# The first five steps of a pipelined attention kernel, with their work in another order

## The chip, the cores and the metric

The kernel runs on one core of a Trainium2 chip. A core has five engines with a queue each, which work through their own instructions in order and wait for one another by semaphores: TensorE (PE; its weight loads are listed as PEld), VectorE (DVE), ScalarE (ACT), GpSimd (POOL) and SyncE (SP), which here issues all transfers. The metric is the device time of one execution in microseconds. Four runs of the kernel before gave 1517.66 to 1519.4 us, median 1518.58 us.

## The reference, cut to what matters

The input x has 16 sequences of 256 tokens with 256 features. The layer is attention with 16 heads of 128, and a feed-forward part whose weights come packed in four bits:

```
x = x + layernorm(attention(layernorm(x)))
x = x + layernorm(ffn(layernorm(x)))
attention:  q, k, v = x W_Q + b_Q, x W_K + b_K, x W_V + b_V     (per head)
            scores = q k / sqrt(128), causal mask, softmax
            out = sum over heads of (softmax v) W_O, + b_O
ffn:        (gelu_tanh(x Wg) * (x Wu)) Wd, weights unpacked from 4 bits and scaled
```

Everything is float32. The kernel keeps that precision by splitting each factor into a rounded high part and the rest, the low part, and adding three products.

## The kernel before

Tokens are taken in blocks of 512 (two sequences), and heads in pairs. A unit is one block with one head; a pair p is one block with two heads, units 2p and 2p+1. There are 128 units. The attention phase is one loop over i from -5 to N+1 (line 1021), a pipeline written out by hand: iteration i works on unit i+5's keys and queries (`st_qk`, line 370), unit i+4's scores and softmax (`st_s`, line 421), its transpose (`st_t`), a fourth part of the values of four heads (`st_v`), the transfers that bring the transposed softmax to the right partitions (`st_w` writes it to DRAM as hop, `st_b` reads it back as pt), the split of pt into ph and pl (`st_p`), the product with the values (`st_z`), and the output product of a finished pair (`st_o`). In the first five iterations most of the later stages have nothing to do yet. From i = 0 on `st_z` runs too, and from the second pair on `st_o`.

Nothing reorders this. The helper `run` (line 95) chains every instruction behind the one emitted before it, and `dma` (line 86) chains every transfer on SyncE, so each engine's order is the order in which the Python code calls. Work that is not part of the pipeline stands in lists of jobs (`splits`, `urgent`, `behind`, `idle` and others). A call of `slot(kinds, lists)` (line 133) advances a counter and lets the first job that is due and of the right kind do one step at that place in the order.

Before the loop the first block's x is normalized, transposed by TensorE and split into xT (`first_tokens`, line 245). TensorE is kept busy meanwhile by transposes of the identity into a tile called warm (`keep_warm`, line 1003).

In `st_qk` six products go into the bank pk; ScalarE adds the bias and writes kh (rounded) and kr (plain), VectorE writes kl, the rest. The same follows with pq, qh, qr and ql. pk and pq have one bank each. In `st_s` TensorE multiplies Q and K into two banks sc, VectorE adds the mask and takes the minima (the scores carry a minus sign) of four pieces, ScalarE takes four exponentials with their sums, VectorE the reciprocals rc in two steps, and GpSimd multiplies pr by them in four. Between the exponentials and the second reciprocal there is a `slot` (line 451). VectorE then transposes pr into tr (`st_t`). `st_v` writes vh by ScalarE and puts VectorE's step for vl into a list called `after`; the next `st_s` runs it behind its minima.

A weight of the first block is split by `w_split` (line 297): ScalarE writes the high part from raw, the low part is written by GpSimd for v and o (all but the first v) and by VectorE for k and q, the next pair's raw is fetched by `w_raw`, and four slots later `w_keep` copies both parts to DRAM, from where later blocks read them. q's weights are multiplied by `qscale` in the same step. `w_get` (line 331) puts such a split on the list `splits`. Before the loop the splits of v's third weight (2) and of k and q for pair 1 are put there, in that order (line 1013); the loop adds k and q of pair p+4 in even iterations, o and v in odd ones. `weights` is the helper that does that (line 1016).

The order in an iteration of the kernel before:

```
if 0 <= i + 4 < N:
    st_s(i + 4)
slot(V_)
if i + 5 < N:
    st_qk(i + 5)
slot(V_, urgent, behind); slot(G_); slot(G_)
if 0 <= i + 4 < N:
    st_t(i + 4)
...  (st_o, st_z, st_p, st_v, st_b, st_w)
weights(...)
slot(A_ + G_)
```

Of the kernel before, what the change touches and what calls it, by code (L numbers as in the profile page):

```python
# [15 lines left out]
ALU = mybir.AluOpType  # L16
# [12 lines left out]
def kernel(  # L29
# [19 lines left out]
    nc = tc.nc  # L49
# [10 lines left out]
    def f(ap):  # L60
        return ap.bitcast(F32)
# [33 lines left out]
    def run(op, dst, *args, **kw):  # L95
        with ExitStack() as behind:
            for m in last.values():
                behind.enter_context(tc.issue_after(m))
            ins = op(dst, *args, **kw)  # L99
        last[ins.ins.engine] = ins.ins  # L100
        return ins
# [3 lines left out]
    V_, G_, A_, N_ = "vgan"  # L105
    urgent, behind, splits, idle, made, spare = (deque() for _ in range(6))
# [3 lines left out]
    def step(jobs, kinds=None):  # L110

        while jobs:
            job, at, kind = jobs[0]
            if kinds and (at > now[0] or kind not in kinds + N_):
                return False
            try:
                to = next(job)
                jobs[0][1:] = (now[0] + to[1], to[0]) if isinstance(to, tuple) else (now[0] + 1, to)
            except StopIteration:
                jobs.popleft()  # L120
            if not kinds or kind != N_:
                return True
        return False

    def add(jobs, job, kind):
        jobs.append([job, 0, kind])

    def overdue(time):
        while late and late[0][0] <= time:
            _, do, args = late.popleft()  # L130
            do(*args)

    def slot(kinds, *lanes):

        now[0] += 1
        overdue(now[0])
        for jobs in lanes or (splits, urgent, behind, made, spare, idle):
            if step(jobs, kinds):
                return
# [149 lines left out]
    def w_tile(n):  # L289
        return wp.tile([P, 2, 1024 if n == "v" else 512], F32R, tag=f"w{n}", name=f"w{n}", bufs=2)  # L290
# [6 lines left out]
    def w_split(p, n):  # L297

        raw = RAW.pop((p, n)).rearrange("p (k c) -> p k c", k=2)
        key, done = p, True  # L300
        if n == "v":
            key, done = p // 2, p % 2
            w = HALF.pop(key) if done else w_tile(n)
            if not done:
                HALF[key] = w
            wv_ = w_view(w)[:, :, :, (p % 2) * 256 : (p % 2 + 1) * 256]
        else:
            w = w_tile(n)
            wv_ = w_view(w)
        c = qscale if n == "q" else 1.0  # L310
        run(nc.scalar.activation, wv_[:, 0], raw, AF.Copy, scale=c)
        if n in "vo" and (p, n) != (0, "v"):
            run(nc.gpsimd.tensor_tensor, wv_[:, 1], raw, f(wv_[:, 0]), ALU.subtract)
        else:
            run(nc.vector.scalar_tensor_tensor, wv_[:, 1], raw, c, f(wv_[:, 0]), ALU.mult, ALU.subtract)
        ahead = p + (2 if n == "v" else 1)
        if ahead < NG:
            w_raw(ahead, n)
        if done:
            W[key, n] = w_view(w)  # L320
            late.append((now[0] + 4, w_keep, (key, n, w)))
# [9 lines left out]
    def w_get(p, n):  # L331

        if p < NG:
            add(splits, split(p, n), A_ if n in "vo" else V_)
        elif p < len(pairs):
            overdue(now[0] + 4)
            if n == "v":
                key, part = p // 2, p % 2
                w = HALF.pop(key) if part else w_tile(n)
                HALF[key] = w  # L340
                dma(f(w[:, part]), WD[key % (NG // 2), n][:, part])
                if part:
                    W[key, n] = w_view(HALF.pop(key))
            else:
                w = w_tile(n)
                dma(f(w), WD[p % NG, n])
                W[p, n] = w_view(w)
# [16 lines left out]
    N = len(units)  # L364
# [3 lines left out]
    after = deque()  # L368
# [52 lines left out]
    def st_s(u):  # L421
        qh, ql, qr = Q.pop(u)
        kh, kl, kr = K.pop(u)
        pr = work.tile([P, 3, 2, P], F32, tag="pr", name="pr")
        mn = small.tile([P, 2, 2], F32, tag="mn", name="mn")
        sm = small.tile([P, 2, 2], F32, tag="sm", name="sm")
        rc = small.tile([P, 2, 2], F32, tag="rc", name="rc")
        parts = ((0, slice(0, 1)), (1, slice(1, 3)))
        scb = []
        for bi in range(2):  # L430
            sc = ps.tile([P, 3 * P], F32, tag="sc", name="sc", bufs=2)
            ks = slice(bi * S, (bi + 1) * S)
            run(nc.tensor.matmul, sc[:, 0:P], qr[:, bi, :], kr[:, bi, :], start=True, stop=True)
            mm3(sc[:, P:], [(lambda a: (qh, ql)[a][:, bi, :], lambda c: (kh, kl)[c][:, ks])])
            for q, cs in ((0, slice(0, P)), (1, slice(P, 3 * P))):
                run(
                    nc.vector.tensor_tensor_reduce,
                    sc[:, cs], sc[:, cs], mask[:, 2 * P - (cs.stop - cs.start) :], scale=1.0, scalar=3.0e38,
                    op0=ALU.add, op1=ALU.min, accum_out=mn[:, bi, q : q + 1],
                )  # L440
            scb.append(sc.rearrange("p (a c) -> p a c", a=3))
        while after:
            run(*after.popleft())
        for bi in range(2):
            for q, cs in parts:
                run(
                    nc.scalar.activation, pr[:, cs, bi, :], scb[bi][:, cs, :], AF.Exp,
                    bias=mn[:, bi, q : q + 1], scale=-1.0, accum_out=sm[:, bi, q : q + 1],
                )
            if bi:  # L450
                slot(V_, splits, idle, urgent, behind)
            run(nc.vector.reciprocal, rc[:, bi, :], sm[:, bi, :])
            for q, cs in parts:
                run(
                    nc.gpsimd.tensor_scalar, pr[:, cs, bi, :], pr[:, cs, bi, :], rc[:, bi, q : q + 1], 1.0,
                    ALU.mult, ALU.mult,
                )
        PR[u] = pr
# [12 lines left out]
    def st_w(u):  # L471
        HOP[u] = dram.tile([P, 4, 6 * 32], F32, tag="hop", name="hop", bufs=4)
        spread(HOP[u], TR.pop(u).rearrange("p k m i -> p k (m i)"))
# [529 lines left out]
    def keep_warm(count):  # L1003
        for n in range(count):
            run(nc.tensor.transpose, warm[:, n % 4, :], ident, ident)

    keep_warm(30)
    add(urgent, first, V_)
    finish(urgent)
    run(nc.gpsimd.tensor_scalar, bqs, bqk[:, 0, :], qscale, 1.0, ALU.mult, ALU.mult)  # L1010
    for p in range(2):
        w_split(p, "v")
    for p, n in (2, "v"), (1, "k"), (1, "q"):
        w_get(p, n)

    def weights(*of):
        for pn, n in of:
# [3 lines left out]
    for i in range(-5, N + 2):  # L1021
        p = i // 2
        odd = i % 2 == 1
        if p >= 0 and not odd and p < len(pairs):
            b, g = pairs[p]
            if g == 0 and b + 1 < NBLK:
                add(urgent, ln1(b + 1), N_)
            if b == 0 and g == 6:
                pieces = [(fg, n) for fg in range(NG) for n in "gud"]
                f_load(*pieces[0])  # L1030
            if b == 0 and g == 7:
                for m, piece in enumerate(pieces):
                    add(idle, f_make(*piece, pieces[m + 1] if m + 1 < len(pieces) else None), V_)
            if b == NBLK - 1 and g == 0:
                add(spare, x_ops(0), N_)
        if 0 <= i + 4 < N:
            st_s(i + 4)
        slot(V_)
        if i + 5 < N:
            st_qk(i + 5)  # L1040
        slot(V_, urgent, behind)
        slot(G_)
        slot(G_)
        if 0 <= i + 4 < N:
            st_t(i + 4)
        if i == N:
            await_(X[0], "last", spare)
            X[0].pop("last")()
        if i >= N - 4:
            part(0, ("m1", "m2", "m6", "m5", "m7", "m3")[i - (N - 4)])  # L1050
        if 0 <= p - 1 < len(pairs):
            st_o(p - 1, i % 2)
        if 0 <= i < N:
            st_z(i)
        if 0 <= i + 1 < N:
            st_p(i + 1)
        if 0 <= i + 4 < N:
            st_v(i + 4)
        elif after:
            run(*after.popleft())  # L1060
        if 0 <= i + 3 < N:
            st_b(i + 3)
        if 0 <= i + 4 < N:
            st_w(i + 4)
        if odd:
            weights((p + 1, "o"), (p + 5, "v"))
        else:
            weights((p + 4, "k"), (p + 4, "q"))
        slot(A_ + G_)
        if N - 9 <= i < N - 7:  # L1070
            f_get(0, "ug"[i - (N - 9)])
# [97 lines left out]
```

## Time and profile before

| | |
|---|---|
| median of four runs | 1518.58 us |
| the profiled execution | 1518.14 us, its span 1516.4 us |
| TensorE busy | 1499.0 us |
| VectorE, ScalarE, GpSimd busy | 1186.4, 1038.4, 731.0 us |
| TensorE busy in 0:10, 10:20, 20:30, 30:40, 40:50 us | 8.36, 7.70, 8.77, 8.82, 10.00 us |
| GpSimd busy in the same | 2.96, 4.64, 3.25, 3.88, 7.28 us |
| share of the 16 DMA engines in the same | 0.73, 0.94, 0.92, 1.00, 1.01 |
| granted TensorE clock | 1.00 in each of these |

The last four rows are busy times in windows of 10 us from the start of the span. Matmuls overlap, so that a busy TensorE is not TensorE at its peak. In a line of the timeline the first number is the start and the second the time in us that the instruction took, or the merged row of several; "xT<-tpx" reads "writes xT from tpx"; what stands in brackets is how long the engine sat idle before it and who ended that. All engines pipeline a little, so that the next instruction may start shortly before the one before it has ended. Nearly every instruction is issued by the helper `run`, and so has line 99; the names of the tiles tell them apart.

### The profile page before, as it was taken

The numbers are of one execution on the slowest core, as the hardware profiler recorded it, in microseconds if no ns is written. First come the engines' busy times: TensorE is split into PE (matmuls) and PEld (weight loads), VectorE is DVE, ScalarE is ACT, GpSimd is POOL, SyncE is SP. The second block draws the span as 40 slices with busy tenths as digits, with TensorE's granted clock in tenths as the row PEclk, the third lists the DMA queues.
The fourth block names the chain that finished last, engine by engine and source line by source line (L and its number), as shares of the span: only waits on it lengthen the run. The fifth ranks groups of instructions, "written<-read, shape, count | busy, mean of one in ns | idle before, by whom it ended". The sixth has DMA issues, their size and how long they took to land.

```text
span 1516.4 us, 25754 instructions
## 1 busy us (share of the span) xinstructions
PE 1499.0 (99%) x7831; PEld 1278.5 (84%) x7831; DVE 1186.4 (78%) x3011; ACT 1038.4 (68%) x2614; POOL 731.0 (48%) x951
## 2 busy tenths in 40 slices
PE   8999999999999999999999999999999999999997
PEld 7888888888888888888888888887888888888886
DVE  6776787787787888788778777777787887787866
ACT  6877766767676677676777767775766665666565
POOL 3755578677667776866876876880000000000000
PEclk9999999999999999999999999999999999999999
DMA  8998899989899899889889999976557465655561
GB/s 300 335 324 260 261 309 309 289 301 309 286 290 329 281 321 301 280 309 314 275 283 321 297 299 317 315 243 263 210 193 262 183 248 196 249 181 195 222 234 57
DMA packets 200426, 407.55 MB, mean 269 GB/s; under 512 B 21472, under 2 KB 128480, under 8 KB 189536
## 3 DMA queue, kind: packets, MB, share of 16 engines
q1 hardware_dynamic: 200288, 405.91, 79.3%
q8 instruction: 62, 1.02, 0.3%
q14 instruction: 76, 0.62, 0.1%
HBM read 294.15 MB, written 111.67 MB: 268 GB/s over the span
## 4 chain that ended last, share of the span: by engine, by line
PE 93%; DVE 2%; DMA 2%; ACT 1%; POOL 1%; issue 1%; SPq 0%; POOLq 0%; DVEq 0%; ACTq 0%
PE pd L99 13%; PE pk L99 11%; PE pv L99 11%; PE pq L99 11%; PE po L99 11%; PE pz L99 10%; PE sc L99 9%; PE pa L99 8%; PE pf L99 5%; PE pe L99 2%; DVE sum L99 1%; DMA wu<-fu 1%; DMA rawq<-in_wq 0%; ACT pr L99 0%; DMA rawv<-in_wv 0%
## 5 line engine op out<-in xcount | busy, mean ns | idle before, releaser
L99 POOL TENSOR_SCALAR pr<-pr,rc 128x128 f32<-128x128 f32 (+1 forms) x512 | 251.5, 507 | 90.3 <-DVE rc L99 90.3
L99 POOL TENSOR_TENSOR rs<-rs,mhalf 128x4 f32<-128x4 f32 (+1 forms) x35 | 34.5, 986 | 485.9 <-DVE rs L99 277.2
L99 ACT ACTIVATE pr<-sc,mn 128x128 f32<-128x128 f32 (+1 forms) x512 | 208.8, 420 | 87.3 <-DVE mn L99 87.3
L99 POOL TENSOR_TENSOR pl<-pt,ph 128x512 fp32r<-128x512 f32 x128 | 165.2, 1291 | 188.6 <-ACT ph L99 184.9
L99 DVE CUSTOM_DVE_ANT_0 sc<-sc,mask 128x128 f32<-128x128 f32 (+1 forms) x512 | 180.7, 373 | 67.8 <-PE sc L99 59.1
L99 PE MATMUL pv<-wv,xT 128*128 128x512 f32 x768 | 208.9, 407 | 0.0
L99 ACT ACTIVATE zh<-pz,bqk 128x512 fp32r<-128x512 f32 x128 | 88.3, 690 | 167.2 <-PE pz L99 167.2
L99 PE MATMUL pk<-xT,wk 128*128 128x512 f32 x768 | 199.5, 395 | 0.3 <-POOL xT L99 0.2
L99 PE MATMUL pd<-inter,wd 128*128 128x512 f32 (+1 forms) x792 | 197.8, 385 | 1.4 <-ACT inter L99 1.0
L99 PE MATMUL pq<-xT,wq 128*128 128x512 f32 x768 | 196.3, 391 | 0.0
L99 PEld LDWEIGHTS pd<-inter,wd 128*128 128x128 f32 x792 | 145.0, 188 | 34.5 <-DVE inter L99 2.9
L99 PEld LDWEIGHTS pq<-xT,wq 128*128 128x128 f32 x768 | 144.2, 188 | 32.9
L99 ACT COPY part<-pa 128x512 f32<-128x512 f32 x192 | 111.9, 586 | 68.7 <-PE pa L99 66.3
L99 PE MATMUL po<-zh,wo 128*128 128x512 f32 x512 | 157.7, 389 | 0.0
L99 PEld LDWEIGHTS pk<-xT,wk 128*128 128x128 f32 x768 | 134.9, 188 | 23.8 <-POOL xT L99 0.7
L99 PEld LDWEIGHTS pv<-wv,xT 128*128 128x128 f32 x768 | 135.0, 189 | 23.6
L99 DVE SCALAR_TENSOR_TENSOR zl<-pz,bqk,zh 128x512 fp32r<-128x512 f32 x128 | 95.9, 749 | 73.4 <-ACT zh L99 73.4
L99 ACT CAST inter<-sum 128x512 fp32r<-128x512 f32 x128 | 80.1, 626 | 87.3 <-DVE sum L99 87.3
L99 DVE TENSOR_TENSOR inter<-sum,inter 128x512 fp32r<-128x512 f32 x128 | 89.1, 696 | 56.9 <-ACT inter L99 55.9
L99 DVE STREAM_TRANSPOSE tr<-pr 128x768 f32<-128x768 f32 x128 | 123.3, 963 | 1.7 <-POOL pr L99 1.2
L99 DVE SCALAR_TENSOR_TENSOR kl<-pk,bqk,kh 128x512 fp32r<-128x512 f32 x128 | 96.1, 751 | 30.8 <-ACT kr L99 27.0
L99 PEld LDWEIGHTS po<-zh,wo 128*128 128x128 f32 x512 | 96.0, 188 | 19.9
(149 smaller groups left out, 3723.7 us busy)
## 6 DMA issues: line engine op xcount, KB each, us to landing
hop<-tr SPq DMA_DIRECT2D x512, 96.0 KB
pt<-hop SPq DMA_DIRECT2D x128, 384.0 KB
wk<-wk SPq DMA_DIRECT2D x64, 512.0 KB
wq<-wq SPq DMA_DIRECT2D x64, 512.0 KB
wo<-wo SPq DMA_DIRECT2D x64, 512.0 KB
wu<-fu SPq DMA_DIRECT2D x32, 1024.0 KB
wg<-fg SPq DMA_DIRECT2D x32, 1024.0 KB
wv<-wv SPq DMA_DIRECT2D x56, 512.0 KB
```

What stands on the lines that cost most here:

```text
L99: ins = op(dst, *args, **kw)
```

## The change

Only the first five iterations (i from -5 to -1), units 0 to 3 of the softmax, and the weights of k and q for pairs 1 to 3 are touched, and the number of warm-up transposes in front.

- In these iterations the products of K and Q for unit i+5 are emitted in front of the scores of unit i+4, no longer behind them. VectorE's steps for vl that the iteration before put into `after` are emitted in front of that.
- Two slots for splits follow behind `st_s`. The slot inside `st_s`, between the exponentials and the second reciprocal, is left out for units 0 to 3.
- For pairs 1 to 3 the low parts of k's and q's weights are written by GpSimd. q's raw weights are first multiplied by `qscale` in place, by one more GpSimd instruction.
- The split of v's third weight is put on the list at the end of iteration -4, and not before the loop. k and q of pair 1 are left on the list before the loop.
- 27 warm-up transposes in place of 30.

```diff
@@ w_split
-        if n in "vo" and (p, n) != (0, "v"):
+        if n in "vo" and (p, n) != (0, "v") or n in "kq" and 1 <= p <= 3:
+
+            if n == "q":
+                run(nc.gpsimd.tensor_scalar, raw, raw, c, 1.0, ALU.mult, ALU.mult)
             run(nc.gpsimd.tensor_tensor, wv_[:, 1], raw, f(wv_[:, 0]), ALU.subtract)
@@ st_s
-            if bi:
+            if bi and u >= 4:
                 slot(V_, splits, idle, urgent, behind)
@@ before the loop
-    keep_warm(30)
+    keep_warm(27)
...
-    for p, n in (2, "v"), (1, "k"), (1, "q"):
-        w_get(p, n)
+    for n in "kq":
+        w_get(1, n)
@@ the loop
+        if i < 0:
+
+
+            while after:
+                run(*after.popleft())
+            st_qk(i + 5)
         if 0 <= i + 4 < N:
             st_s(i + 4)
+        if i < 0:
+            for _ in range(2):
+                slot(V_, splits)
         slot(V_)
-        if i + 5 < N:
+        if 5 <= i + 5 < N:
             st_qk(i + 5)
...
+        if i == -4:
+            w_get(2, "v")
         if odd:
             weights((p + 1, "o"), (p + 5, "v"))
```

## The prediction

> **What bounds the kernel now.** I read the page first. TensorE is busy for all but 17.4 us of the span, so work taken from another engine is worth nothing where TensorE doesn't wait for it.
>
> ```profile
> PE 1499.0 (99%) x7831; PEld 1278.5 (84%) x7831; DVE 1186.4 (78%) x3011; ACT 1038.4 (68%) x2614; POOL 731.0 (48%) x951
> PE 93%; DVE 2%; DMA 2%; ACT 1%; POOL 1%; issue 1%; SPq 0%; POOLq 0%; DVEq 0%; ACTq 0%
> ```
>
> Then I read the waits of the first 50 us (columns: who <- for whom: us, times, longest). The change touches nothing after them. The only wait of TensorE behind the launch is four times for the last part of Q, 4.7 us in all. After 39.17 it runs without a gap worth naming.
>
> ```profile
> PE sc L99 <- ACT qr L99: 4.7, 4, 1.5
> ```
>
> Last, the timeline of one early iteration (i = -1, unit 3's softmax beside unit 4's products).
>
> ```profile
> 33.74 0.27 DVE L99 CUSTOM_DVE_ANT_0 sc<-sc,mask 128x128 f32<-128x128 f32 x1
> ...
> 34.68 0.37 ACT L99 ACTIVATE pr<-sc,mn 128x128 f32<-128x128 f32 x1 [1.64 <-DVE mn L99]
> ...
> 35.63 0.17 DVE L99 RECIPROCAL rc<-sm 128x2 f32<-128x2 f32 x1 [0.27 <-ACT pr L99]
> ...
> 35.89 0.83 POOL L99 TENSOR_SCALAR pr<-pr,rc 128x128 f32<-128x128 f32 x2 [3.84 <-DVE rc L99]
> ...
> 36.28 0.64 ACT L99 ACTIVATE wk<-rawk 128x512 fp32r<-128x512 f32 x1
> ...
> 36.80 0.64 ACT L99 ACTIVATE wq<-rawq 128x512 fp32r<-128x512 f32 x1
> ...
> 37.33 0.69 ACT L99 ACTIVATE kh<-pk,bqk 128x512 fp32r<-128x512 f32 x1
> ...
> 38.42 0.75 DVE L99 SCALAR_TENSOR_TENSOR kl<-pk,bqk,kh 128x512 fp32r<-128x512 f32 x1
> 38.61 0.51 ACT L99 ACTIVATE qr<-pq,bqs 128x256 f32<-128x256 f32 x1
> ...
> 39.17 0.49 PE L99 MATMUL sc<-kr,qr 128*128 128x128 f32 x2 [1.12 <-ACT qr L99]
> ...
> 39.55 0.97 DVE L99 STREAM_TRANSPOSE tr<-pr 128x768 f32<-128x768 f32 x1
> ...
> 39.70 1.29 POOL L99 TENSOR_TENSOR pl<-pt,ph 128x512 fp32r<-128x512 f32 x1 [0.70 <-ACT ph L99]
> ...
> 40.95 1.31 POOL L99 TENSOR_TENSOR wo<-rawo,wo 128x512 fp32r<-128x512 f32 x1
> ...
> 42.59 1.64 POOL L99 TENSOR_SCALAR pr<-pr,rc 128x128 f32<-128x128 f32 x4 [0.34 <-DVE rc L99]
> ```
>
> The ring is: minima, exponentials, the next pair's weights, the next unit's K and Q on ScalarE, scores, minima. Call M(u) the start of unit u's minima. In the trace M(0) to M(5) are 14.02, 21.44, 28.08, 33.74, 40.44 and 46.73. The reader should also see that GpSimd multiplies pr, then has pl and wo, and has room.
>
> **The change part by part.** Step lengths are from rows of the trace: minima to exponentials 0.94 (33.74 to 34.68); exponentials to first reciprocal 0.95, to GpSimd 0.26, its four multiplications 1.64: M to the end of pr 3.79, so the transpose starts 3.9 after M if nothing else holds it. Transpose to the next VectorE step 0.89 (39.55 to 40.44), vl 0.61, kl 0.73, ql 0.40. On ScalarE the exponentials take 1.60, wk and wq 1.05, kh, kr, qh 0.57, 0.36, 0.36, qr 0.51 to its end.
>
> *Three warm-ups fewer.* Thirty weight loads take 5.30 us (1.57 to 6.87), three 0.53. The transposes of x behind them waited for the loads by 0.4, then wait for the layer norm on VectorE. I take 0.2 earlier for the first product (9.01 to 8.8); the ends are 0 and 0.5.
>
> *K and Q in front of the scores.* TensorE now does pk(1), pq(1) before sc(0). pk has one bank, so pk(1) waits for kl(0): kr(0)'s end 11.56 (11.76 less 0.2) plus 0.75 is 12.3. Then pk 1.28 (28.01 to 29.29), the time from pq's first load to qh 1.85 (10.27 to 12.12), qr's end 0.87 later, ql 0.4: M(0) = 16.8, where it was 14.02. This is 2.8 us paid at once. In return the scores no longer wait for Q. But on VectorE, which runs in order, kl and ql of the next unit leave the place where they lay beside GpSimd's multiplications, and stand behind the transpose and in front of the minima. The new ring is 3.9 + 0.89 + 0.73 + 0.40 = 5.92, not the 5.66 of M(2) to M(3) before.
>
> *vl in front.* In i = -3 and -2 the low part of V comes behind the transpose too: 0.61, ring 6.53. M(1) = 16.8 + 6.53 = 23.3. For M(2) ScalarE is longer: exponentials at 24.3, then 1.60, wk and wq 1.05, vh 0.46, wv 0.54, then kh to qr's end 1.80 gives 29.75, and ql: M(2) = 30.2. M(3) = 36.1. Then i = 0 has the old order, scores before products, so M(4) = 36.1 + 3.9 + 0.89 = 40.9 against 40.44. The ring alone loses 0.45.
>
> *v's third weight later.* Before, ScalarE waited 2.2 us for its transfer in front of the first exponentials (they began at 15.70). That wait goes, which is in the sum above: the first transpose would be at 20.7, where it was 20.55. The load that this split issues moves from 12.90 to about 23.4 on SP; its data is used at 46.49.
>
> *Weights split behind the minima, low parts on GpSimd.* k's and q's low parts leave VectorE (0.69 and 0.67, three times), where they stood beside GpSimd's multiplication, and cost it 0.29 (1.12 against 0.83 for a pair). GpSimd gets k's low part at 1.25 (39.70 to 40.95, same shape), q's scaling and q's low part at 1.25. The scaling, 128x512 in place by two constants, isn't in the trace. The nearest row is pr's: 0.37 for 128 and 0.48 for 256 elements in one pair of 0.83, from which I work out 0.69 for 512; the far end is xn's, 1.23 for 256, so 2.46; below is 0.4, two rows of 0.2 as bqs has. I take 0.69, for pr's is the same operation. In i = -5 the three hide behind pk(1), pq(1) (done by 16.7, needed at 17.6 by pk(2)); in i = -3 they end at 30.4, and pq(4) begins at 31.5. In i = -1 nothing hides them: GpSimd runs in order, and pl(0), wo(0) and pr(4) are queued behind. pr(3) ends at 39.9, k's low 41.15, scaling 41.85, q's low 43.1, pl(0) 44.4 (was 41.0), wo 45.65, pr(4) 47.3 (was 44.23). Then transpose, zl (0.63): M(5) = 47.35 + 0.89 + 0.63 = 48.9, against 46.73. TensorE itself is ahead by 1.0 at 42, then waits about 2.2 for pl(0) in pz(0) (its first two products need no pl), so sc(5) starts at 46.9 against 45.58. sc(6) follows M(5) by the old ring: 52.18 + 2.15 = 54.3. By TensorE's own work it would be 53.4, so M(5) decides. From there on the work of TensorE per unit (7.73, 52.18 to 59.91) is longer than the ring, the lag of 2.1 stays, and the later idle time (mostly waits for ACT, DVE and POOL at the change of phase) moves with it.
>
> *SP's queue.* The copies of k and q to DRAM, and q's next load, now wait on SP for GpSimd's low parts. Queued behind are pt and hop: pt(0) is issued at about 30.8 where it was 26.30. With the 5.4 us that it took to land, that is 36.2, and ScalarE wants it at 39.75: hidden, with 3.5 to spare. pt(2) and pt(3) have 5 us each. If that cover goes, every us beyond is a us of delay.
>
> Sum: 2.1 us. The profiled execution's span 1516.4 becomes 1518.5; with the 1.7 around it (1518.14) 1520.2. It was 0.4 below the median 1518.58, so 1520.7.
>
> [...] No row here shows the scaling itself.
>
> **The rivals.** *A, the scores' wait simply goes.* The 4.7 us and the 0.2 of warm-ups are gained: 1513.7. For it: TensorE needs only 5.3 per early unit. Against: VectorE's ring of 5.9 to 6.5. It decides if rings come out at 5.3 or less and pl(0) ends before 42. *B, GpSimd's queue costs nothing,* since its steps overlap or pr(4) isn't last: the ring's 0.45 stays, 1519.0. *C, the scaling is slow:* at 2.46 it adds 1.8 to the same chain, 3.9 in all, 1522.5; from 1.6 on it is slower by over 0.2%. *D, SP's queue:* transfers run at a share of 1.00 from 30 to 40, and if pt(0) lands at 42 in place of 36.2, ScalarE stands 2.2 longer in front of the exponentials of unit 4: 1522.9.
>
> **How the numbers follow.** Forecast 0.48, A 0.12, B 0.14, C 0.18, D 0.08. My three rings may each be off by 0.5, so the forecast's own range is 1519.2 to 1522.3. 0.2% is 3.0 us, about what a measurement of this kernel can tell from no change: under 1515.5 is faster, over 1521.6 slower. A quarter of the forecast (0.12) lies above, with C and D 0.38; A is faster, 0.12; the rest 0.50. The range, 1517.0 to 1523.4, takes in B with its rings' error and C and D nearly whole, and leaves out A and the tails, 0.2.
>
> **What would show it.** Right: scores no longer wait for qr before unit 5; M(0) near 16.8, M(3) near 36; pz waits some 2 us for pl near 42; GpSimd without a gap from pr(3) to pr(4). Wrong: M(3) under 35 or pl(0) done before 42 (then A or B), a scaling over 1.2 us (C), ScalarE idle before ph for a transfer (D).

## The result, and the profile after

The changed kernel takes 1520.66 us (median of 41 runs) where the kernel before takes 1518.93 us (61 runs beside them). The ratio is 1.0011, with an interval of 1.0006 to 1.0015: some 0.9 to 2.3 us slower. The forecast was 1520.7 us, and a time within 0.2% of before as the likeliest outcome, at 0.50. Both hold. The steps in between held less evenly, and two of them were wrong.

The page of the changed kernel, its busy times and the shares of its chain:

```profile
PE 1500.2 (99%) x7828; PEld 1279.2 (84%) x7828; DVE 1182.2 (78%) x3005; ACT 1038.5 (68%) x2614; POOL 739.6 (49%) x960
PE 93%; DVE 3%; ACT 1%; POOL 1%; issue 1%; DMA 1%; SPq 0%; POOLq 0%; DVEq 0%; ACTq 0%
```

Nine more instructions on GpSimd, six fewer on VectorE (its share of the chain went from 2% to 3%) and three transposes fewer on TensorE: the change does what it says. The waits of the first 55 us (who <- for whom: us in total, times, longest) show what became of TensorE's wait for Q, which was four times and 4.7 us:

```profile
DVE tr L99 <- POOL pr L99: 5.5, 5, 1.7
...
PE sc L99 <- ACT pr L99: 2.2, 1, 2.2
...
PE pv L99 <- DVE vl L99: 1.1, 2, 0.8
...
PE sc L99 <- ACT qr L99: 0.8, 1, 0.8
...
PE pz L99 <- POOL pl L99: 0.3, 1, 0.3
```

The scores no longer wait for Q in the first five units. In their place VectorE waits five times for GpSimd's multiplications, and TensorE waits for the exponentials (the scores of unit 4 need the bank that those of unit 3 still hold), for vl, and for Q once more at unit 6. One ring, on VectorE, as the prediction describes it (unit 1's transpose to unit 2's minima; behind each line in brackets is the idle time before it):

```profile
26.84 0.98 DVE L99 STREAM_TRANSPOSE tr<-pr 128x768 f32<-128x768 f32 x1 [0.97 <-POOL pr L99]
27.75 0.65 DVE L99 TENSOR_TENSOR vl<-pv,vh 128x512 fp32r<-128x512 f32 x1
28.70 0.75 DVE L99 SCALAR_TENSOR_TENSOR kl<-pk,bqk,kh 128x512 fp32r<-128x512 f32 x1 [0.30 <-ACT kr L99]
29.43 0.48 DVE L99 SCALAR_TENSOR_TENSOR ql<-pq,bqs,qh 128x256 fp32r<-128x256 f32 x1
29.83 0.29 DVE L99 CUSTOM_DVE_ANT_0 sc<-sc,mask 128x128 f32<-128x128 f32 x1
```

vl, kl and ql now stand between the transpose and the minima, and the 0.30 in front of kl is ScalarE being longer in this one ring. GpSimd's queue from unit 3's multiplications to unit 4's:

```profile
37.77 1.64 POOL L99 TENSOR_SCALAR pr<-pr,rc 128x128 f32<-128x128 f32 x4 [4.12 <-DVE rc L99]
39.38 1.29 POOL L99 TENSOR_TENSOR wk<-rawk,wk 128x512 fp32r<-128x512 f32 x1
40.75 0.62 POOL L99 TENSOR_SCALAR rawq<-rawq 128x512 f32<-128x512 f32 x1
41.45 1.28 POOL L99 TENSOR_TENSOR wq<-rawq,wq 128x512 fp32r<-128x512 f32 x1
42.70 1.28 POOL L99 TENSOR_TENSOR pl<-pt,ph 128x512 fp32r<-128x512 f32 x1
43.94 1.28 POOL L99 TENSOR_TENSOR wo<-rawo,wo 128x512 fp32r<-128x512 f32 x1
45.20 1.64 POOL L99 TENSOR_SCALAR pr<-pr,rc 128x128 f32<-128x128 f32 x4
```

There is no gap in it, and what follows it on VectorE starts as soon as it is done:

```profile
46.87 0.98 DVE L99 STREAM_TRANSPOSE tr<-pr 128x768 f32<-128x768 f32 x1 [1.67 <-POOL pr L99]
47.77 0.71 DVE L99 SCALAR_TENSOR_TENSOR zl<-pz,bqk,zh 128x512 fp32r<-128x512 f32 x1
48.40 0.29 DVE L99 CUSTOM_DVE_ANT_0 sc<-sc,mask 128x128 f32<-128x128 f32 x1
```

So M(5) is 48.40, where it was 46.73. The first weight load of the scores of unit 6 follows it by 5.45 us in both kernels, and from there the changed kernel stays behind by 1.67 us through the whole attention phase.

In units of the prediction, the starts of the minima:

| | M(0) | M(1) | M(2) | M(3) | M(4) | M(5) |
|---|---|---|---|---|---|---|
| before | 14.02 | 21.44 | 28.08 | 33.74 | 40.44 | 46.73 |
| predicted | 16.8 | 23.3 | 30.2 | 36.1 | 40.9 | 48.9 |
| after | 16.74 | 23.05 | 29.83 | 35.60 | 40.35 | 48.40 |

The new order pays 2.7 us at M(0), earns it back by M(4), and loses it again between M(4) and M(5), behind GpSimd.

One thing in this trace is in no part of the prediction: TensorE's granted clock. The windows of 5 us (length, busy us and instructions of PE, PEld, DVE, ACT and POOL, then the clock, the share of the DMA engines, GB/s):

```profile
35.00:40.00 5.00, 2.83 (x15) 2.16 (x14) 3.07 (x13) 3.43 (x12) 2.23 (x5) 0.93 0.93 337
40.00:45.00 5.00, 4.72 (x21) 3.73 (x19) 3.25 (x13) 4.24 (x14) 4.83 (x5) 0.73 0.96 332
```

Behind the wait of 2.2 us in front of the scores of unit 4 the clock was granted at 0.50, from 39.27 to 42.69. The products of K and Q for unit 5 took 2.54 and 2.15 us in that stretch:

```profile
37.53 0.49 PE L99 MATMUL sc<-kr,qr 128*128 128x128 f32 x2 [2.17 <-ACT pr L99]
...
39.02 2.54 PE L99 MATMUL pk<-xT,wk 128*128 128x512 f32 x6
41.37 2.15 PE L99 MATMUL pq<-xT,wq 128*128 128x512 f32 x6
...
44.03 0.39 PE L99 MATMUL pz<-pl,vh 128*128 128x256 f32 x1 [0.28 <-POOL pl L99]
```

Two theories came out of this. The first is the prediction's: the rings on VectorE set M(0) to M(4), and GpSimd's queue sets M(5) and with it the lag. The second: the half clock, or the new gap in front of it, sets the lag, and GpSimd's queue only happens to end at the same time. A third question was what each part of the change is worth by itself.

### The profile page after: what moved, and what is told of

It is laid out like the page before. It is cut to its first block, busy times and chain, and to the rows that moved or that the text cites. A ratio compares the mean times of both kernels' runs of the same rounds, so it can differ in the third digit from the quotient of the medians.

```text
span 1517.2 us, 25756 instructions
## 1 busy us (share of the span) xinstructions
PE 1500.2 (99%) x7828; PEld 1279.2 (84%) x7828; DVE 1182.2 (78%) x3005; ACT 1038.5 (68%) x2614; POOL 739.6 (49%) x960
## 4 chain that ended last, share of the span: by engine, by line
PE 93%; DVE 3%; ACT 1%; POOL 1%; issue 1%; DMA 1%; SPq 0%; POOLq 0%; DVEq 0%; ACTq 0%
PE pd L99 13%; PE pk L99 11%; PE po L99 11%; PE pq L99 11%; PE pv L99 11%; PE pz L99 10%; PE sc L99 9%; PE pa L99 8%; PE pf L99 5%; PE pe L99 2%; DVE sum L99 1%; PE warm L99 0%; POOL pr L99 0%; DMA hop<-tr 0%; ACT pr L99 0%
```

## The experiments

Each kernel was timed beside the kernel before on the same chip. The lag is how much later the kernel does the same instruction in the attention phase than the profiled run of before does. Profiled runs start between 0.2 us earlier and 0.9 later than that of before, and not at one moment even where the code up to there is the same; the lag below has that taken off, by the first kh of each run (for the changed kernel 1.67 becomes 1.85). Lags and M come from one profiled run each, medians and ratios from the timed runs. The two don't always agree: the lag of e4_scores_first is -0.99 and its median 2.85 below before, the lag of e2_lows_vector 1.60 and its median 0.29 above. So a difference of less than 2 us between two of these kernels rests on the lag, where their intervals overlap.

| kernel | M(3) | M(4) | M(5) | lag | median, us | before beside it | ratio, 95% |
|---|---|---|---|---|---|---|---|
| changed | 35.60 | 40.35 | 48.40 | 1.85 | 1520.66 | 1518.93 | 1.0011, 1.0006 to 1.0015 |
| e1_pair3_vector | 35.85 | 41.58 | 47.86 | 1.09 | 1519.19 | 1519.38 | 0.9998, 0.9989 to 1.0007 |
| e2_lows_vector | 36.23 | 41.96 | 48.25 | 1.60 | 1519.67 | 1519.38 | 1.0002, 0.9993 to 1.0011 |
| e3_lows_alone | 34.00 | 40.69 | 47.11 | 0.59 | 1520.84 | 1519.38 | 1.0009, 1.0001 to 1.0018 |
| e4_scores_first | 32.05 | 37.71 | 46.03 | -0.99 | 1516.53 | 1519.38 | 0.9982, 0.9973 to 0.9991 |
| f1_pair3_later | 32.04 | 37.70 | 45.02 | -0.47 | 1517.32 | 1519.58 | 0.9987, 0.9978 to 0.9996 |
| f2_pair3_later_gpsimd | 31.59 | 37.25 | 43.90 | 1.97 | 1521.13 | 1519.58 | 1.0013, 1.0004 to 1.0022 |
| f3_scaling_thrice | 36.29 | 41.04 | 50.50 | 3.30 | 1522.10 | 1519.58 | 1.0016, 1.0007 to 1.0025 |
| f4_vl_behind | 41.77 | 46.51 | 54.55 | 7.96 | 1525.65 | 1519.58 | 1.0046, 1.0034 to 1.0059 |
| g1_pair3_old_place | 31.51 | 38.20 | 44.48 | -2.07 | 1517.20 | 1519.38 | 0.9987, 0.9978 to 0.9996 |
| g2_v4_later | 30.77 | 37.46 | 43.74 | -1.93 | 1516.87 | 1519.38 | 0.9987, 0.9978 to 0.9996 |
| g3_gap_filled | 35.92 | 40.66 | 48.69 | 1.82 | 1520.82 | 1519.38 | 1.0011, 1.0002 to 1.0020 |
| g4_v_later_alone | 33.23 | 39.93 | 46.22 | -1.37 | 1518.04 | 1519.38 | 0.9994, 0.9985 to 1.0003 |

### Does GpSimd's queue set the end? Two scalings more in it

The first theory says that every us added in front of pl(0) and pr(4) comes out at the end.

```diff
@@ w_split of the changed kernel
                 run(nc.gpsimd.tensor_scalar, raw, raw, c, 1.0, ALU.mult, ALU.mult)
+                for _ in range(2 if p == 3 else 0):
+                    run(nc.gpsimd.tensor_scalar, raw, raw, 1.0, 1.0, ALU.mult, ALU.mult)
```

> The changed kernel with two more multiplications by one of the same size behind q's scaling, for pair 3 alone. Theory G, that the chain of GpSimd from pr(3) to pr(4) sets M(5) and with it the end: each costs 0.69 to 0.71, M(5) 49.8 instead of 48.4, 1.4 us slower than the changed kernel, 3.1 slower than before. If another engine sets it, no change against the changed kernel.

The same stretch of GpSimd's timeline:

```profile
41.45 2.04 POOL L99 TENSOR_SCALAR rawq<-rawq 128x512 f32<-128x512 f32 x3
43.58 1.28 POOL L99 TENSOR_TENSOR wq<-rawq,wq 128x512 fp32r<-128x512 f32 x1
44.81 1.27 POOL L99 TENSOR_TENSOR pl<-pt,ph 128x512 fp32r<-128x512 f32 x1
46.03 1.28 POOL L99 TENSOR_TENSOR wo<-rawo,wo 128x512 fp32r<-128x512 f32 x1
47.30 1.64 POOL L99 TENSOR_SCALAR pr<-pr,rc 128x128 f32<-128x128 f32 x4
```

Two scalings more are 1.42 us more (2.04 against 0.62). The lag grew by 1.45, from 1.85 to 3.30. The chain pr, low parts, pl, wo, pr sets M(5), one for one, and M(5) sets the lag. The medians, 1522.10 against 1520.66, each beside its own runs of before, agree with this, but the intervals of their ratios overlap.

### Does the half clock set it? The gap filled

```diff
@@ the loop of the changed kernel, iteration 0
+        if i == 0:
+            keep_warm(18)
         if 0 <= i + 4 < N:
             st_s(i + 4)
```

> The changed kernel with 18 transposes of the identity in the gap of TensorE in front of sc(4). Theory G: the granted clock stays 1.00, pk(5) and pq(5) take 1.5 each instead of 2.5 and 2.15, but pz(0) then waits about 2 us for pl(0) instead of 0.3; M(5) stays 48.4 and the time is the changed kernel's. Rival C, the half clock costs: M(5) and the time fall by 1.5 us.

With 18 transposes in the gap, the granted clock is 1.00 in both windows, where the changed kernel had 0.93 and 0.73. The windows of this run:

```profile
35.00:40.00 5.00, 4.83 (x35) 4.15 (x34) 3.08 (x13) 3.12 (x12) 1.90 (x5) 1.00 0.98 335
40.00:45.00 5.00, 3.14 (x17) 2.55 (x17) 3.25 (x12) 4.56 (x15) 4.83 (x5) 1.00 0.98 336
```

and TensorE's timeline (the view begins at 36, and 16 of the 18 transposes are in it):

```profile
35.77 1.91 PE L99 MATMUL warm<-ident 128*128 128x128 f32 x16
...
39.34 1.54 PE L99 MATMUL pk<-xT,wk 128*128 128x512 f32 x6
40.72 1.52 PE L99 MATMUL pq<-xT,wq 128*128 128x512 f32 x6
...
44.33 0.39 PE L99 MATMUL pz<-pl,vh 128*128 128x256 f32 x1 [1.86 <-POOL pl L99]
```

K's and Q's products take 1.54 and 1.52 again, and TensorE spends what this saves waiting for pl(0): 1.86 in place of 0.28. The lag is 1.82, that of the changed kernel, and so is the ratio, 1.0011. The second theory falls: the half clock filled a wait that was there anyway.

### Without GpSimd's low parts

One kernel gives only pair 3's low parts back to VectorE, the other those of all three pairs.

```diff
@@ w_split, e1_pair3_vector
-        if n in "vo" and (p, n) != (0, "v") or n in "kq" and 1 <= p <= 3:
+        if n in "vo" and (p, n) != (0, "v") or n in "kq" and 1 <= p <= 2:
@@ w_split, e2_lows_vector
-        if n in "vo" and (p, n) != (0, "v") or n in "kq" and 1 <= p <= 3:
+        if n in "vo" and (p, n) != (0, "v"):
```

> The changed kernel, but the low parts of k and q for pair 3 on VectorE again (pairs 1 and 2 stay on GpSimd). Theory G, GpSimd's queue in iteration -1 makes the lag: GpSimd goes from pr(3) straight to pl(0), pl(0) ends near 41.2 instead of 44.0 and pr(4) near 44.9 instead of 46.8; VectorE pays two low parts in front of the transpose, M(4) 41.1 instead of 40.35; M(5) 47.4 instead of 48.4, sc(6) 52.85 instead of 53.85; about 1.0 us faster than the changed kernel, 0.7 slower than before. Rival C, the half clock of TensorE from 39 to 43 makes the lag: the gap before sc(4) stays, so the clock falls again, M(5) stays 48.4 and the time is the changed kernel's.

> The changed kernel, but all low parts of k and q on VectorE again, no scaling: the new order alone. Theory G: VectorE pays 0.4 in iteration -3 and 0.75 in -1, M(2) 30.2, M(4) 41.5, M(5) 47.8, about 1.05 slower than before and 0.6 faster than the changed kernel. If GpSimd's low parts were the only fault of the change, this one would be faster than before. If they were no fault, it would be slower than the changed kernel by the 1.4 per pair on VectorE, 2 us or more.

GpSimd's queue in e1_pair3_vector ends earlier (pl(0) at 41.90, pr(4) at 45.36), and yet the lag falls only from 1.85 to 1.09. Its timeline shows why, first GpSimd's:

```profile
38.02 2.62 POOL L99 TENSOR_SCALAR pr<-pr,rc 128x128 f32<-128x128 f32 x4 [4.12 <-DVE rc L99]
40.61 1.29 POOL L99 TENSOR_TENSOR pl<-pt,ph 128x512 fp32r<-128x512 f32 x1
```

and VectorE's at the same time:

```profile
39.09 0.69 DVE L99 SCALAR_TENSOR_TENSOR wk<-rawk,wk 128x512 fp32r<-128x512 f32 x1 [0.35 <-ACT wk L99]
39.70 0.68 DVE L99 SCALAR_TENSOR_TENSOR wq<-rawq,wq 128x512 fp32r<-128x512 f32 x1
40.68 0.98 DVE L99 STREAM_TRANSPOSE tr<-pr 128x768 f32<-128x768 f32 x1 [0.30 <-POOL pr L99]
```

While VectorE writes two low parts, GpSimd's four multiplications take 2.62 us and not 1.64. The first three of the four take 1.16 us in the changed kernel (1.64 less the 0.48 of the last), which here would end them at 39.18, 0.09 behind the start of VectorE's first low part; so the excess of 0.98 lies in the fourth, by this estimate. The four end at 40.64, 0.26 behind the second low part. The transpose waits for them, so M(4) is 41.58 and not 40.35. Low parts on VectorE make the ring longer; low parts on GpSimd make the queue in front of M(5) longer. In e2_lows_vector the slow multiplications come in two iterations (2.62 at 25.29 and at 38.40) and the lag is 1.60, almost that of the change. The three kernels' times lie too near each other to be told apart by their intervals; by the medians alone e1 and e2 lie 1.5 and 1.0 us below the change.

### GpSimd's low parts alone

```diff
@@ w_split of the kernel before
-        if n in "vo" and (p, n) != (0, "v"):
+        if n in "vo" and (p, n) != (0, "v") or n in "kq" and 1 <= p <= 3:
+            if n == "q":
+                run(nc.gpsimd.tensor_scalar, raw, raw, c, 1.0, ALU.mult, ALU.mult)
```

> The kernel before, only with the low parts of k and q for pairs 1 to 3 on GpSimd, with the scaling. Theory G: in the old order the splits begin before the products of Q, so GpSimd has k's low part between its multiplications and q's behind them, beside kl and ql; T(u) is still held by ql; pl(0) ends near 42.3 where pz(0) asks for it at 43.4, pr(4) near 45.2; M(5) 46.8, no change within 0.3 us. If GpSimd's 3.2 us per pair cost in any order, it is 1.5 us or more slower than before.

In the old order k's low part lies between the two pairs of multiplications, where GpSimd had room. pr(4) ends at 45.55 (before 44.23), and the lag is 0.59. Most of it doesn't come from there: with the start taken off, M(1) is 0.29 late and M(2) to M(4) are 0.46 to 0.47 late, and pr(4) adds 0.13 to that. The expectation, no change within 0.3 us, missed this. The median is 1.5 above before. In its profiled run the lag grows by 2.95 us more near 1049 us, where TensorE waits 1.5 us for wu's transfer, which is told of at the end.

### The products back behind the scores, and v's third weight later

In e4_scores_first the order of scores and products, and of vl, is the old one; the split of v's third weight, the two slots behind, the slot left out in `st_s` and GpSimd's low parts stay as in the change. g4_v_later_alone has only v's third weight moved.

```diff
@@ the loop, e4_scores_first against the changed kernel
-        if i < 0:
-            while after:
-                run(*after.popleft())
-            st_qk(i + 5)
         if 0 <= i + 4 < N:
             st_s(i + 4)
+        slot(V_) if i >= 0 else None
+        if i + 5 < N:
+            st_qk(i + 5)
         if i < 0:
             for _ in range(2):
                 slot(V_, splits)
-        slot(V_)
-        if 5 <= i + 5 < N:
-            st_qk(i + 5)
+            slot(V_)
```

```diff
@@ g4_v_later_alone against the kernel before
-    for p, n in (2, "v"), (1, "k"), (1, "q"):
+    for p, n in (1, "k"), (1, "q"):
         w_get(p, n)
...
+        if i == -4:
+            w_get(2, "v")
```

> The changed kernel with K's and Q's products and vl where they stood before (scores first); the later split of v, the splits behind the products, GpSimd's low parts and 27 warm-ups stay. Theory R, that the products in front lengthen VectorE's ring: M(0) 13.8, M(1) 19.5, M(2) 25.2, M(3) 31.5, M(4) 37.1, then GpSimd's queue of k, q, pl, wo holds pr(4) to 44.2 and M(5) to 45.8: about 2.6 us faster than the changed kernel and 1.0 faster than before. If the products in front are a gain that GpSimd hides, it is slower than the changed kernel.

> The kernel before with v's third weight split at the end of iteration -4, nothing else. ScalarE no longer waits 2.2 us for its load in front of the first exponentials; they start at 14.95 instead of 15.70, and everything behind, M(1) to M(5) and sc(6), comes 0.7 earlier. If the first iteration is held by VectorE or GpSimd anyway, M(1) stays 21.4.

With the scores first the lag turns from 1.85 into -0.99, and the kernel is faster than before: 0.9982, 0.9973 to 0.9991. Products and vl in front thus cost 2.8 us by the lag, about what M(0) paid at once (by the medians 4.1). Here too the ring is ahead at M(4) (37.71, before 40.44), and GpSimd's queue takes 2 us of that back: M(5) is only 0.70 ahead. v's third weight later is worth 1.37 by the lag; 0.89 of that is the later start of this one run, so that between 0.5 and 1.4 is what its trace shows. Its ratio, 0.9994 with 0.9985 to 1.0003, doesn't reach beyond no change. No run has the moved slots alone.

### vl behind

```diff
@@ the loop of the changed kernel
-            while after:
-                run(*after.popleft())
             st_qk(i + 5)
```

> The changed kernel with vl behind the minima again. If vl in front only lengthens VectorE's ring, M(1) and M(2) come 0.6 earlier each and the time falls by up to 1 us. By the trace pv's bank waits for vl on TensorE, which does pv(1) in front of pk(3): then M(1) is 22.4, but vl(0) ends at 24.6 instead of 22.1, pk(3) starts 26.0 instead of 23.6, M(2) is 30.5, vl(1) holds pv(2) until 32.6, M(3) is 37.6, and it is 2 us slower than the changed kernel.

The waits of the first 55 us:

```profile
PEld pv L99 <- DVE vl L99: 5.8, 2, 3.1
PE pv L99 <- DVE vl L99: 5.4, 2, 2.9
```

The mechanism was as expected, and the price was not: the lag is 7.96, some 6 above that of the change. The value product waits for the bank of pv until vl has been taken behind the minima, TensorE stands still for 2.90 and 2.47 us, and in the windows behind these gaps (25 to 30 and 35 to 40) the granted clock is 0.66, where it is 1.00 in the windows with the gaps (20 to 25 and 30 to 35). The six products of V behind the first gap take 2.79 us and those of K behind the second 2.56, where the six of Q at 29.26 take 1.53. Here the slowed products lie in the ring, and M(2) to M(3) is 9.6 us; how much of that is the wait and how much the clock, no run separates. So taking vl first belongs to the order with the products in front.

### Versions with e4's order

Since GpSimd's queue still takes 2 us there, pair 3's low parts were moved: to VectorE in iteration 0 (f1_pair3_later), to GpSimd in iteration 0 behind the products of unit 5 (f2_pair3_later_gpsimd), and back to VectorE at their old place, between the exponentials and the second reciprocal (g1_pair3_old_place). g2_v4_later also puts off v's fourth weight by an iteration.

```diff
@@ f1_pair3_later against e4_scores_first (pair 3 not on GpSimd, not on the list at i = -2)
+        if i == 0:
+            for n in "qk":
+                splits.appendleft([split(3, n), 0, V_])
@@ f2_pair3_later_gpsimd against e4_scores_first (pair 3 not on the list at i = -2)
             st_qk(i + 5)
+        if i == 0:
+            for n in "kq":
+                w_split(3, n)
@@ g1_pair3_old_place against e4_scores_first (pair 3 not on GpSimd)
-            if bi and u >= 4:
+            if bi and u >= 3:
                 slot(V_, splits, idle, urgent, behind)
...
-        slot(V_) if i >= 0 else None
+        slot(V_) if i >= -1 else None
@@ g2_v4_later against g1_pair3_old_place
-        if i == -4:
-            w_get(2, "v")
+        if i in (-4, -2):
+            w_get(i // 2 + 4, "v")
         if odd:
-            weights((p + 1, "o"), (p + 5, "v"))
+            weights((p + 1, "o"), (p + 5 if i > -3 else 0, "v"))
```

> Scores first as in e4, and pair 3's k and q split not in iteration -1 but in iteration 0, inside st_s and in front of st_qk, low parts on VectorE. Theory G: GpSimd goes from pr(3) to pl(0), wo and pr(4) without the 3.2 us of pair 3, pr(4) ends near 41.5; M(4) 37.3, M(5) 44.6, sc(6) 50.0: 2.1 us faster than before, 1.1 faster than e4. If e4's M(5) was held by something else than GpSimd, M(5) stays near 46.

> Scores first as in e4, pair 3's k and q split in iteration 0 behind st_qk(5), low parts on GpSimd behind pr(4). Theory G with the ring of ScalarE: the high parts leave the ring, M(5) 43.6, and pl(1) near 46.6 is in time for pz(1) at 47.7; pr(5) waits for wv until 47.9 but its transpose is held by ql anyway; sc(6) near 49.2, where TensorE's own work ends: 2.9 us faster than before. If GpSimd's low parts cost wherever they are, sc(6) is no earlier than in f1.

> Scores first as in e4; pair 3's k and q are split in iteration -1 as in the kernel before, inside st_s and in front of st_qk, low parts on VectorE, so that pair 4's loads are issued as early as before. Theory G: M(3) to M(4) takes 6.7 as before, M(4) 38.75, GpSimd is free for pl(0) and pr(4), M(5) 45.0, sc(6) 50.5 without a wait for weights: 1.7 us faster than before at sc(6), 1.0 faster than e4. If the loads of pair 4 are late here too (as in f1, f2), sc(6) is near 52.

> As g1, and v's fourth weight split one iteration later (-2). In e4 pr(2) waited for its low part on GpSimd and M(2) to M(3) took 6.5. With it out of the way 5.7: M(3) 31.2, M(4) 37.9, M(5) 44.2, sc(6) 49.7: 2.5 us faster than before, 0.8 faster than g1. If M(3) is held by ScalarE or TensorE instead, it is g1's.

f1 and f2 come within 0.4 us of the M(5) that was expected (45.02 and 43.90), and lose it one unit later. The split of a pair also issues the load of the next pair's raw weight, and a later split means a later load. ScalarE's timeline in f1_pair3_later:

```profile
49.67 0.63 ACT L99 ACTIVATE wq<-rawq 128x512 fp32r<-128x512 f32 x1 [1.19 <-DMA rawq<-in_wq]
```

and in f2_pair3_later_gpsimd:

```profile
49.51 0.63 ACT L99 ACTIVATE wk<-rawk 128x512 fp32r<-128x512 f32 x1 [2.92 <-DMA rawk<-in_wk]
```

Behind these stand the next K and Q, so the scores of unit 6 start at 52.02 and 52.51 (before 52.18), and in f2 the products of K behind the gap take 2.05 us, where those of the unit before took 1.56. f2, expected to be 2.9 us faster than before, is 1.5 us slower by the medians.

g1 keeps the loads where they were: M(5) is 44.48, TensorE doesn't wait for pl, and the lag of -2.07 stays. Its ratio, 0.9987 with 0.9978 to 0.9996, is faster than both kernels, as e4's is. g2 is ahead by 0.74 more at M(5) and ends at -1.93, a little behind g1. It loses the gain in a similar way: v's transfers now lie in SP's queue from 36.68 to 38.61, in place of 31.38 to 32.31; behind them the load of the next block's x is issued at 47.21 and not at 44.56 as in g1, and VectorE stands waiting for it in front of the transpose. That the first makes the second late is read from the queue's order and not tested. Its timeline:

```profile
51.33 0.75 DVE L99 BATCH_NORM_STATS2 st<-xs 128x6 f32<-128x256 f32 x2 [1.68 <-DMA xs<-in_x]
52.00 0.96 DVE L99 STREAM_TRANSPOSE tr<-pr 128x768 f32<-128x768 f32 x1
```

e4, g1 and g2 can't be told apart by their times. By the lag g1 should beat e4 by 1.1 us, and by the medians e4 is ahead by 0.7; this stays open.

## Why the prediction was right, and where it wasn't

*The sum.* Predicted 2.1, measured 1.67 in the profiled run (1.85 with the start taken off) and 1.73 between the medians. What ends it is the step that the prediction said: M(5), behind GpSimd. f3_scaling_thrice shows it and g3_gap_filled excludes the nearest other reading. That the median, 1520.66, falls on 1520.7 is luck: the sum was 0.4 too large, and the kernel before came out 0.35 slower beside it than in the four runs that the forecast started from.

*K and Q in front.* M(0) was 16.8 and came at 16.74, by the working that was given: one bank for pk, so that pk(1) waits for kl(0) (0.57 us). The terms of that working add up to 16.7; 16.8 is a slip of 0.1. "2.8 us paid at once" was 2.72, and the difference between e4 and the change is 2.8 in all.

*The rings.* "M to the end of pr 3.79, so the transpose starts 3.9 after M" was the mis-sized term: the transposes came 3.79 to 3.85 after M, right behind GpSimd. In three rings that is 0.05 to 0.1 each; with VectorE's steps in between about 0.1 shorter than summed, M(3) is 0.5 earlier than predicted, and that 0.5 is the whole difference at M(5) too. M(2) by ScalarE was right in kind (0.30 of idle time in front of kl) and 0.4 late in size. "The ring alone loses 0.45" was thus about nothing: M(4) came at 40.35 against 40.44.

*GpSimd's queue.* From the end of pr(3) to M(5) the prediction had 9.0 us; the trace has 8.99 (39.41 to 48.40). The scaling, not in the trace of before, was taken at 0.69 and took 0.62, 0.70 to the next instruction; the bounds, 0.4 and 2.46, were 0.2 and 1.8 off. The choice of the nearest row, the same operation at a smaller size, was right.

*"pz waits some 2 us for pl."* Wrong in the changed kernel: 0.28. In its place the clock was granted at 0.50 from 39.27 to 42.69, and K's and Q's products took 2.54 and 2.15 us, against 1.54 and 1.52 at 1.00 in g3_gap_filled. The step that failed is "TensorE itself is ahead by 1.0 at 42": it left out that TensorE might run slower behind its wait of 2.2 us, as it did here. g3_gap_filled has the wait for pl at 1.86, so the step is nearly right with the clock at 1.00, and no time hangs on it.

*"In return the scores no longer wait for Q."* They don't before unit 5, as was said, but TensorE waits 2.2 us for the exponentials that hold the scores' banks. The prediction's sum went by M and so took it in, but it didn't name this wait.

*Three warm-ups fewer.* "0.2 earlier" matches the first kh of the profiled run (0.18 earlier) by chance: other kernels with 27 warm-ups began between 0.19 earlier and 0.47 later than before, and e3_lows_alone, with 30, 0.21 earlier. No run here isolates its worth.

*SP's queue.* pt(0) was predicted to be issued at 30.8 and to land at 36.2. It was issued at 30.60 and landed at 35.02; ScalarE took it at 39.21. The cover held, and so D didn't come about.

*What the low parts cost on VectorE.* The prediction had read in the trace of before that a low part there slows a pair of GpSimd's multiplications by 0.29 (1.12 against 0.83), and for the new order without them it had the ring alone losing 0.45. With all of them on VectorE the lag is 1.60 (e2_lows_vector; its median, 0.29 above before with an interval of -1.1 to 1.7, doesn't decide it): two low parts slowed four multiplications by 0.98 (2.62 against 1.64), and these are in the ring. Why the multiplications take longer beside VectorE's low parts, no run shows.

*The rivals.* A needed rings of 5.3 or less; they came at 5.8 to 6.8. B needed GpSimd's queue to cost nothing; f3 shows that it costs one for one. C needed a scaling of 1.6; it took 0.62. What none of them held: a part of A's gain was there to be had. g1_pair3_old_place, with -2.07, has the old order of scores and products, so that M(0) isn't paid for, together with the later split of v and the low parts of pairs 1 and 2 on GpSimd.

## What to carry to other kernels

Follow one round of the pipeline and ask, for each instruction that is moved, which engine's in-order queue it now stands in front of; here TensorE's wait for Q vanished, and in its place VectorE waits for GpSimd, to which work had been pushed (five times, 5.5 us). A step that is moved takes its DMA issues along, and the stage that starves may be a unit or two later (f1 and f2 lost their gain in that way, and by the order of the queue g2 too). Of a change of several parts, try the parts alone: here, by the lag, one weight's later split gains 0.5 to 1.4 us by itself, and the products in front, on which the change is built, cost 2.8.

## What the runs showed of the hardware

*The clock after a gap.* In the changed kernel TensorE loads no weights for 2.60 us in front of the scores of unit 4, and the clock is granted at 0.50 from 39.27 to 42.69, 3.4 us; with 18 transposes in that gap it is 1.00 (g3_gap_filled). In f4_vl_behind it is 0.66 in the windows behind waits of 2.90 and 2.47 us. e1_pair3_vector has a gap of 2.6 us in front of the same scores, and a clock of 1.00 from 35 to 45; the kernel before has gaps of up to 1.9 us in front of its scores, and 1.00 in each window of its first 50 us. So a gap of one length comes with the slower clock in one run and without it in another; the length alone doesn't decide, and what else does, no run shows.

*A transfer far from the change.* Near 1049 us, at the start of the feed-forward part, the products pa wait for wu's transfer in some of the profiled runs: 0.6 us in before, 1.0 in e4_scores_first, 1.5 in g3_gap_filled and in e3_lows_alone, and not in the changed kernel. The lag changes there in each profiled run by another amount: by -0.83 in the changed kernel, +0.53 in e4_scores_first, +1.00 in g4_v_later_alone, +1.66 in g3_gap_filled, and +2.95 in e3_lows_alone. That is why the span of the changed kernel's profiled run is only 0.8 us above before's (1517.2 and 1516.4), and it is as large as most differences in the table. What decides when that transfer lands wasn't found out.
